# Two graph layers on one core: the prologue's order of bias rows and of the bound check's squarings

## Chip, cores and metric

The kernel runs on one NeuronCore of a Trainium2 chip. The metric is the device time of one execution in microseconds, as the median of three runs. The profile is of one further execution, taken by the hardware profiler.

## What is computed

The input `x` holds 64 samples of 256 nodes with 512 features; `adj` is one 256 x 256 adjacency matrix for all samples. Two layers follow each other, each with a layer norm and a ReLU ahead of it and a residual around it. The first is a graph attention with one head, the second an attention with eight heads of 64, masked by `adj`. All is in float32. Cut to what matters:

```python
h = maximum(layernorm(x), 0)
hw = h @ W                                   # 512 -> 256
e  = leaky_relu(hw @ a[0] + (hw @ a[1]).T, 0.2) + NEG * (1 - adj)
x  = x + concatenate([softmax(e) @ hw, hw])
h = maximum(layernorm(x), 0)
q, k, v = h @ Wq.T + bq, h @ Wk.T + bk, h @ Wv.T + bv      # 8 heads
s = where(adj == 0, -inf, q @ k.T / 8)
x = x + (softmax(s) @ v) @ Wo.T + bo
```

## The kernel before

**Tiling.** Samples go in groups of two (`GB`), so there are 32 groups (`NG`). A group's rows are four tiles of 128 rows by 512 features. While one group is in attention, the next one is projected and the one after that is in the first layer. A loop over the groups at the end of `bounded` does this, with its order written as strings of letters; ahead of it stands a prologue that brings the first groups up to that point. The change lies in the prologue (lines 1133 to 1169).

**Seven products instead of eight.** Each projection (q, k, v), and the output projection too, is done on a 2 x 2 split of its operands with seven block products and sums of blocks. So the weights need four extra blocks (`weight_sums`, line 253: T3, T1, T2, T4; T1 overwrites the block W12), and the activations three sums (`operand_sums`, line 525, on GpSimd). `projection` (line 851) issues the products in the order 1, 2, 6, 7, 5, 4, 3. They are `pq`, `pk` and `pv` in the profile, eight recorded matmuls each. ScalarE moves three of the banks on as `kept_q`, `kept_k`, `kept_v` and the last as `q`, `k` or `v`; VectorE adds three (`q<-pq,kept_q`). Product 6 accumulates onto product 1's bank, so it has to wait for the copy of that. The seventh product of k uses the bank that q's last product has been taken from.

**Norm and transposition.** `norm_T` (line 428) measures rows, makes scale and shift (`factor`, VectorE and GpSimd), normalizes on ScalarE (`xn`) and transposes. Except for the first group the transposition is done in 32 x 32 blocks by VectorE into `xt` (one buffer), then stored to DRAM (`passed<-xt`) and fetched back in four pieces (`moved<-passed`), and copied by ScalarE to `hT0` (first layer) or `hT` (second layer; both stand as `hT` in the profile). `turn` notes its last transposition in `turn_last`.

**The output bias.** The bias of v goes through the output weights: `last_bias` (line 272) has three steps. The first makes `bv_rows` on VectorE, one scaling and three multiply-adds of 128 x 512 elements, from the four unsummed blocks of `wo_sb`; its first instruction gets an edge to what `turn_last` holds. The second multiplies a matrix of ones by them on TensorE (`pb`). The third adds the result to `b_out`. GpSimd's weight sums of `wo_sb` overwrite a block that the rows read.

**The bound check.** Attention is done without subtracting a row maximum. `judge` (line 293) works out bounds of the weights' norms from which `conclude` decides whether that is allowed. Its steps are the letter "c": a Gram matrix of `wq` per head pair, one of `wk`; then the first squarings (`square_q`, `square_k`: eight recorded matmuls of 128 x 128 each), their copies back to `room` by ScalarE, and the second squarings, of which ScalarE sums the squares (`room<-square_q`). The rest follows late in the kernel.

**What sets the order.** The program is written in the wanted order, and a scheduler at build time gives each engine its fixed sequence. TensorE's is exactly that of the program: `matmul` chains every instruction to the one before (`in_order`, line 131). On the other engines `not_sooner` (line 123) ties an instruction to the engine's last one written so far. What isn't tied may be placed earlier or later by the scheduler. ScalarE's copies of q and k, its normalizations and its copies of `hT` are tied; VectorE's sums of products are not.

**The prologue's loop.** Twenty-one product steps of the first group, q, k and v mixed, are taken by `next(products)`: steps 0 to 3 (q1, q2, k1, k2) ahead of the loop, and then one for each i from 4: q6, q7, q5, q4, q3 (i = 4 to 8), k6, k7, k5, k4, k3 (9 to 13), v1, v2, v6, v7, v5, v4, v3 (14 to 20). Between them each i takes letters of `order`: "n" is a step of the third group's norms, "s" a step of the second group's first layer. At 5 there are the second group's last features (`ph`) and its score rows (`line`, `own`); at 7 its attention weights `e`; at 10 and 11 its four weighed features (`po`, two at each); at 12 and 13 the norm and transposition for its second layer; at 14 and 16 the third group's second normalization and its second transposes; at 17 and 19 the copies to `hT`. In the kernel before, the check's first squarings and copies come at 4, the second squarings at 7, the rows at 16, `pb` at 19 and its sum at 20.

Of the kernel before, what the change touches and what calls it, by code (L numbers as in the profile page):

```python
# [41 lines left out]
def two_gnn_layers(tc, *args):  # L42

    nc = tc.nc
    with tc.tile_pool(name="verdict", bufs=1) as pool:
        wrong = pool.tile([1, 1], I32, name="wrong")
        bounded(tc, *args, wrong)  # L50
        again = nc.values_load(wrong[0:1, 0:1], min_val=0, max_val=1)
        with tc.If(again > 0):
            tc.strict_bb_all_engine_barrier()
            any_inputs(tc, *args)
# [3 lines left out]
def bounded(  # L58
# [64 lines left out]
    def not_sooner(engine, operation, *args, **kwargs):  # L123

        last = engine.last
        after(getattr(engine, operation)(*args, **kwargs), last)
# [25 lines left out]
    def load(g, b):  # L152
        xs[g, b] = big.tile([P, NT, D], F32, tag="x", name=f"x{g}_{b}", bufs=8)
        if g in (2, 3):
            not_sooner(sync, "dma_start", xs[g, b], xg[g, b])
        else:
            sync.dma_start(xs[g, b], xg[g, b])
# [95 lines left out]
    def weight_sums(name, engine=vector):  # L253
        w = w_sb[name]
        not_sooner(engine, "tensor_sub", w[:, :, T3, :], w[:, :, W22, :], w[:, :, W12, :])
        engine.tensor_sub(w[:, :, T1, :], w[:, :, W12, :], w[:, :, W11, :])
        engine.tensor_sub(w[:, :, T2, :], w[:, :, W22, :], w[:, :, T1, :])
        engine.tensor_sub(w[:, :, T4, :], w[:, :, W21, :], w[:, :, T2, :])

    def first_weight_sums():  # L260
        w11, w12, w21, w22 = (
            w0_sb[:, 2 * c : 2 * c + 2, h * FH : (h + 1) * FH] for c in range(2) for h in range(2)
        )
        t2, t3, t4 = (w0_more[:, i] for i in range(3))
        not_sooner(gpsimd, "tensor_sub", t3, w22, w12)
        not_sooner(gpsimd, "tensor_sub", w12, w12, w11)
        not_sooner(gpsimd, "tensor_sub", t2, w22, w12)
        not_sooner(gpsimd, "tensor_sub", t4, w21, t2)
# [864 lines left out]
    def take(*names):  # L1133
        for name in names:
            next(work[name])
# [10 lines left out]
    take(*"n00c0n0n")  # L1146
    late_loads()
    weight_sums("q")
    take(*"uunuu0011")
    order = "nnn ssn n s - s ss ss s s n - n s - s -".split()  # L1150
    for i, parts in enumerate(order, 4):
        next(products)
        if i == 4:
            take(*"ccc")
        if i == 17:
            weight_sums("o", gpsimd)
        if i in (5, 12):
            weight_sums("kv"[i // 12])
        if i == 8 and NG > 3:
            load(3, 0)  # L1160
            load(3, 1)
        if i == 7:
            take(*"cc")
            first_weight_sums()
        for part in parts:
            if part != "-":
                next(norms if part == "n" else pieces, None)
        if i in (16, 19, 20):
            next(bias)
    additions = (piece for g in range(NG) for piece in residual(g))  # L1170

# [3 lines left out]
    for g in range(NG):  # L1175
        products = project(g + 1) if g + 1 < NG else iter(())
        pieces = first_layer(g + 2) if g + 2 < NG else iter(())
        for b, parts in enumerate(steps):
# [10 lines left out]
            i, count = -1, sum(part not in "frv" for part in parts)  # L1189
# [410 lines left out]
```

## Time and profile before

| | us |
|---|---|
| median of three runs (2403.78 to 2406.71) | 2404.09 |
| the profiled execution, its own time | 2403.24 |
| its span | 2401.6 |
| TensorE busy | 2383.5 (99%) |
| VectorE busy | 1696.1 (71%) |
| GpSimd busy | 1423.4 (59%) |
| ScalarE busy | 1021.7 (43%) |
| `bv_rows` begins / `pb` begins | 88.14 / 91.89 |
| first scores (`sc`) begin | 96.33 |

In the profile PE is TensorE, DVE is VectorE, ACT is ScalarE, POOL is GpSimd and SP is the engine that issues the DMAs. A line of the timeline gives the start, the length, the engine, the operation, what it writes and reads, the shapes and how many were merged; in brackets stands the idle time of the engine ahead of it and what ended that. The ends of matmuls are modelled and overlap, so their starts are the better measure. A line of the waits gives the waiting engine, the engine waited for, the total, the number and the longest. The granted clock of TensorE is a share of its full speed. Nearly all operations carry line 35 or 137, those of two helpers, so they are told apart by the names of their tiles.

### The profile page before, as it was taken

To read this page: it belongs to the slowest core of one execution; us is meant where nothing else is said; L and a number is where in the kernel's file an instruction comes from. 1 tells how busy PE (TensorE), PEld (TensorE's weight loads), DVE (VectorE), ACT (ScalarE), POOL (GpSimd) and SP (SyncE) were. 2 spreads that over 40 slices of the span, in tenths; PEclk is the share of its full clock that TensorE was granted. 3 is DMA by queue.
4 is the path that set the end of the run, shared out by engine and by line. 5 is a ranking of instruction groups with operands and counts; after the bars stand their busy time and mean duration, and the time that the engine had idled before them with its cause. 6 is when DMAs were issued, how large, how long until landed. Compare 5 with 4: busy or idle time off the path is not lost.

```text
span 2401.6 us, 43080 instructions
## 1 busy us (share of the span) xinstructions
PE 2383.5 (99%) x15824; PEld 2011.0 (84%) x15824; DVE 1696.1 (71%) x3346; ACT 1021.7 (43%) x2017; POOL 1423.4 (59%) x1290
## 2 busy tenths in 40 slices
PE   9899999999999999999999999999999999999998
PEld 8788888888888888888888888888888888888886
DVE  7586766776766767667767677776677676676655
ACT  4443444444443434444444434344444444343431
POOL 4465656656656565566555575555665565656552
PEclk9999999999999999999999999999999999999999
DMA  6345444544455544455444544444554445554331
GB/s 193 106 136 157 133 147 154 158 145 137 141 158 150 159 143 134 145 154 158 145 141 137 158 150 154 149 134 144 154 158 145 137 142 158 149 158 141 112 105 46
DMA packets 272041, 343.76 MB, mean 143 GB/s; under 512 B 25424, under 2 KB 217168, under 8 KB 271824
## 3 DMA queue, kind: packets, MB, share of 16 engines
q1 hardware_dynamic: 271824, 340.95, 45.9%
q8 instruction: 126, 2.06, 0.4%
q14 instruction: 91, 0.75, 0.1%
HBM read 177.22 MB, written 163.64 MB: 142 GB/s over the span
## 4 chain that ended last, share of the span: by engine, by line
PE 96%; DMA 1%; DVE 1%; ACT 0%; issue 0%; SPq 0%; POOL 0%; ACTq 0%; DVEq 0%
PE py L137 16%; PE pk L137 16%; PE pq L137 16%; PE pv L137 16%; PE sc L137 10%; PE pr L137 9%; PE ph L137 8%; PE po L137 4%; DMA adj_i<-in_adj_dram 0%; DMA moved<-passed 0%; DMA wv_sb<-in_L_gnn_Wv_dram 0%; DMA passed<-xt 0%; DVE xt L35 0%; DVE x L35 0%; ACT hT L35 0%
## 5 line engine op out<-in xcount | busy, mean ns | idle before, releaser
L35 POOL TENSOR_TENSOR p<-p 128x512 f32<-128x512 f32 x248 | 386.2, 1570 | 481.9 <-DVE p L35 464.7
L35 ACT ACTIVATE xn<-x,factor 128x512 f32<-128x512 f32 x256 | 194.8, 807 | 337.2 <-POOL factor L35 328.3
L35 DVE TENSOR_TENSOR p<-p,maskT 128x1024 f32<-128x1024 f32 x254 | 329.7, 1318 | 3.9 <-ACT p L35 3.9
L35 DVE TENSOR_TENSOR x<-py,x 128x256 f32<-128x256 f32 x448 | 185.7, 415 | 185.9 <-PE py L137 179.7
L35 ACT ACTIVATE p<-sc 128x512 f32<-128x512 f32 x512 | 257.7, 627 | 136.0 <-PE sc L137 119.1
L35 POOL TENSOR_TENSOR parts<-parts 128x512 f32<-128x512 f32 x248 | 248.1, 1000 | 84.6 <-DMA parts<-rows 62.0
L137 PE MATMUL py<-wo_sb,oT 128*128 128x256 f32 x1024 | 262.4, 379 | 0.6 <-DVE oT L35 0.6
L137 PE MATMUL sc<-q,k 64*128 64x256 f32 x2048 | 251.5, 390 | 0.3 <-ACT p L35 0.3
L137 PE MATMUL pk<-hT,wk_sb 128*128 128x256 f32 x1024 | 244.9, 382 | 1.5 <-ACT q L35 1.5
L137 PEld LDWEIGHTS sc<-q,k 64*128 64x128 f32 x2048 | 204.5, 186 | 47.9 <-issue 25.9
L137 PE MATMUL pq<-hT,wq_sb 128*128 128x256 f32 x1024 | 240.1, 382 | 1.1 <-ACT hT L35 0.7
L137 PE MATMUL pv<-wv_sb,hT 128*128 128x256 f32 x1024 | 236.8, 379 | 0.0
L137 PE MATMUL pr<-p,v 128*32 128x256 f32 x4096 | 234.2, 380 | 0.0
L137 PEld LDWEIGHTS pq<-hT,wq_sb 128*128 128x128 f32 x1024 | 191.8, 190 | 36.7 <-issue 10.3
L137 PEld LDWEIGHTS pk<-hT,wk_sb 128*128 128x128 f32 x1024 | 189.6, 190 | 35.2 <-issue 9.9
L35 POOL TENSOR_TENSOR factor<-factor,rexp 128x2 f32<-128x2 f32 (+1 forms) x132 | 117.9, 893 | 169.8 <-DVE factor L35 169.5
L137 PEld LDWEIGHTS py<-wo_sb,oT 128*128 128x128 f32 x1024 | 194.1, 190 | 28.2 <-DVE oT L35 1.1
L137 PEld LDWEIGHTS pv<-wv_sb,hT 128*128 128x128 f32 x1024 | 194.5, 190 | 26.5
L137 PEld LDWEIGHTS pr<-p,v 128*32 128x32 f32 x4096 | 126.8, 110 | 97.8 <-issue 16.6
L137 PE MATMUL py<-wo_sb,o_sums 128*128 128x256 f32 x768 | 197.6, 380 | 0.5 <-DVE x L35 0.5
L137 PE MATMUL pv<-wv_sb,sums 128*128 128x256 f32 x768 | 182.4, 380 | 0.8 <-ACT kept_v L35 0.8
L137 PE MATMUL pq<-sums,wq_sb 128*128 128x256 f32 x768 | 181.5, 379 | 0.8 <-POOL sums L35 0.8
(150 smaller groups left out, 4076.1 us busy)
## 6 DMA issues: line engine op xcount, KB each, us to landing
passed<-xt SPq DMA_DIRECT2D x124, 512.0 KB, 3.1
moved<-passed SPq DMA_DIRECT2D x496, 128.0 KB, 3.5
rows<-p SPq DMA_DIRECT2D x124, 512.0 KB, 3.4
parts<-rows SPq DMA_DIRECT2D x496, 128.0 KB, 3.0
x<-in_x_dram SPq DMA_DIRECT2D x64, 512.0 KB, 4.4
out_dram<-x SPq DMA_DIRECT2D x62, 512.0 KB, 3.9
own<-line SPq DMA_DIRECT2D x31, 256.0 KB, 3.1
wq_sb<-in_L_gnn_Wq_dram SPq DMA_DIRECT2D x2, 512.0 KB, 9.0
```

Of the source, the lines that this page charges most:

```text
L35: instruction = getattr(self.engine, operation)(*args, **kwargs)
L137: in_order(nc.tensor.matmul(*args, **kwargs))
```

## The change

Three moves within the prologue; no instruction is added or dropped.

1. The first step of `last_bias`, the rows, is taken at i = 15 instead of 16. At 15 it comes ahead of the "n" of 16, the third group's second transposes, so `turn_last` still holds the transposition of i = 13.
2. The check's first squarings (`square_q`, `square_k`) are taken ahead of the loop, directly behind two features of the second group, and so ahead of product q6. Their copies to `room` stay at 4, behind it.
3. The check's second squarings are taken at i = 11 instead of 7: behind product k5 and the first two weighed features, ahead of the last two.

```diff
-    take(*"uunuu0011")
+    take(*"uunuu0011cc")
     order = "nnn ssn n s - s ss ss s s n - n s - s -".split()
     for i, parts in enumerate(order, 4):
         next(products)
         if i == 4:
-            take(*"ccc")
+            take("c")
         if i == 17:
             weight_sums("o", gpsimd)
         if i in (5, 12):
             weight_sums("kv"[i // 12])
         if i == 8 and NG > 3:
             load(3, 0)
             load(3, 1)
+        if i == 11:
+            take(*"cc")
         if i == 7:
-            take(*"cc")
             first_weight_sums()
         for part in parts:
             if part != "-":
                 next(norms if part == "n" else pieces, None)
-        if i in (16, 19, 20):
+        if i in (15, 19, 20):
             next(bias)
```

## The prediction

> **What bounds the kernel now.** I read the page first, then the waits of TensorE for the first 260 us, then each engine's timeline there.
>
> ```profile
> PE 2383.5 (99%) x15824; PEld 2011.0 (84%) x15824; DVE 1696.1 (71%) x3346; ACT 1021.7 (43%) x2017; POOL 1423.4 (59%) x1290
> ```
>
> TensorE is busy for 99% of the span, and the chain that ended last is 96% PE. What an edit of the prologue can win is therefore time in which PE stands still there, and a microsecond won at 100 us is kept to the end as long as no new wait opens. The waits are few:
>
> ```profile
> PE pb L137 <- DVE bv_rows L35: 5.6, 1, 5.6
> PE pk L137 <- ACT q L35: 1.5, 1, 1.5
> ...
> PE pq L137 <- POOL sums L35: 0.8, 1, 0.8
> PE pv L137 <- ACT kept_v L35: 0.8, 1, 0.8
> ```
>
> The timeline of PE places them (start, length, the wait in brackets):
>
> ```profile
> 44.72 1.99 PE L137 MATMUL pq<-sums,wq_sb 128*128 128x256 f32 x8 [0.83 <-POOL sums L35]
> 46.55 1.05 PE L137 MATMUL square_q<-room 128*128 128x128 f32 x8
> ...
> 57.01 1.05 PE L137 MATMUL square_q<-room 128*128 128x128 f32 x8
> 57.90 1.06 PE L137 MATMUL square_k<-room 128*128 128x128 f32 x8
> 58.79 1.89 PE L137 MATMUL pq<-sums,wq_sb 128*128 128x256 f32 x8
> 60.52 1.89 PE L137 MATMUL pk<-sums,wk_sb 128*128 128x256 f32 x8
> 63.95 1.99 PE L137 MATMUL pk<-hT,wk_sb 128*128 128x256 f32 x8 [1.53 <-ACT q L35]
> ...
> 84.39 1.89 PE L137 MATMUL pv<-wv_sb,hT 128*128 128x256 f32 x8
> 91.89 2.08 PE L137 MATMUL pb<-bv_rows,square_ones 128*128 128x512 f32 x2 [5.61 <-DVE bv_rows L35]
> 93.75 2.65 PE L137 MATMUL pv<-wv_sb,sums 128*128 128x256 f32 x8
> 96.33 3.92 PE L137 MATMUL sc<-q,k 64*128 64x256 f32 x32
> ```
>
> Starts 1.73 us apart are an eight-piece product at full pace. After the long wait it is slower (93.75 to 96.33 is 2.58). The reason for the long wait is VectorE's order:
>
> ```profile
> 79.74 1.29 DVE L35 STREAM_TRANSPOSE xt<-xn 128x512 f32<-128x512 f32 x2
> 84.66 0.69 DVE L35 TENSOR_TENSOR v<-pv,kept_v 128x512 f32<-128x512 f32 x1 [3.63 <-PE pv L137]
> 86.32 0.69 DVE L35 TENSOR_TENSOR v<-pv,kept_v 128x512 f32<-128x512 f32 x1 [0.96 <-PE pv L137]
> 86.92 1.29 DVE L35 STREAM_TRANSPOSE xt<-xn 128x512 f32<-128x512 f32 x2
> 88.14 0.45 DVE L35 TENSOR_SCALAR bv_rows<-wo_sb,bv_col 128x512 f32<-128x512 f32 x1
> ```
>
> The rows stand behind the third group's second transposes (86.92), while VectorE has 3.63 us free from 81.03.
>
> [...] the granted clock falls at 88.45, 2.2 us into the wait, and returns at 95.28, 6.83 us[...] later. [...] ACT's copy of q stands behind the whole attention chain and starts at 63.07, when that ends at 63.16. [...] The last of the four row instructions takes 1.63 us beside GpSimd's weight sums, the two before it 0.75.
>
> **Part 1, the rows one step sooner.** It removes the edge to the transposes of 86.92 and leaves one to those of 79.74. Nothing is added: the four instructions (0.45 + 2 x 0.75 + 1.63, from 88.14 to 91.85 = 3.7 us) move into VectorE's gap, and with them, earlier, GpSimd's three sums of wo_sb that wait for them. Their inputs landed long ago. At the old pace they would end at 81.03 + 3.7 = 84.7; pb is wanted at 84.39 + 1.73 = 86.12. The stall goes: 91.89 - 86.12 = 5.77. The slow clock behind it goes too: pb and one product take 96.33 - 91.89 = 4.44; at full pace 0.86 (pb streams as many columns as half a product) + 1.73 = 2.59; so 1.85. Sum **7.6 us**. No DMA is in this step. Queued behind the rows on VectorE are v's sums (84.66 and 86.32); the last v product needs the bank that the first of them reads, but comes after pb, so 1.6 late is still in time. The store and the loads of the third group's transposes keep their places on SP's queue; if the rows do push those transposes, by 3.7 at most, their operand copies on ACT (106.45) have some 10 us in hand after the loads issued at 88.72. What is late next I come to under part 3.
>
> **Part 2, the first squarings ahead of q's sums.** The 0.83 us wait at 44.72 is for GpSimd; the squarings (16 pieces, 46.55 to 48.34 = 1.79) are ready and fill it. The product then starts at 43.72 + 1.79 = 45.51 and the next ends at 48.97 instead of 50.07: 1.1 us. But ACT has kept_q, two room copies and then hT in fixed order; kept_q follows that product, so starts at 47.4 instead of 46.76, and the first hT copy ends near 47.4 + 0.84 + 2 x 0.55 + 0.6 = 49.9. The features that read it (50.07) can start at 49.95. Bounds 0 to 1.1; I take **0.1**, that is nothing: the wait goes from GpSimd's sums to hT.
>
> **Part 3, the second squarings behind the weighed features.** They were 1.79 us of work ahead of the 63.95 wait, and that wait is not set by PE. It ends with ACT's copy of q, behind the exponentials (61.74 to 63.16), behind own's landing at 60.05, behind the features. ACT loses its two squarings (58.16 to 59.75) but was idle 0.34 for the DMA before e, so the chain does not move. PE now reaches the wait at 62.25 - 1.78 = 60.47 and stands still 3.48 us instead of 1.7. Two costs follow.
> - *The work itself*, now after the wait, ahead of the last two weighed features. These start 1.78 later, and VectorE, which was full from 66.84 to 81.03, idles for them: its reciprocal would come at 72.08 (1.06 after the features, as at 65.78 and 66.84) instead of 70.51, 1.5 later. Then factor, xn, k, kept_v shift by up to 1.53 and the product of 78.81 starts at 80.34; PE alone would be there at 77.88 + 1.78 = 79.66, a shift of 0.85. Between these I take **1.2**. ACT's two squarings (0.6 each and 0.2 to read a sum) now stand ahead of its xn (71.89, which waits for GpSimd's factor until then); they would run between 70 and 72, so xn may lose some 0.2, which the bounds cover. No DMA belongs to these steps.
> - *The clock*. [...] The record has a window with 1.53 idle that kept full clock, and one with 2.17 idle (86.28 to 88.45) that lost it. So the clock most likely halves around 64, for one window: half of 3.41 us, **1.7**. Bounds 0 and 3.4[...].
>
> *What is late next*: the scores. VectorE's transposes of 79.74 feed a store, a load and ACT's hT copy: 81.03 to 90.18, 9.15 us, then v's copy (0.6) and the exponentials. With the transposes shifted by 1.2 to 1.5 the exponentials can start at 92.0 at the soonest, where the scores come at 86.12 + 1.2 + 2.6 = 89.9; they hold five banks and need the first back after two pairs, at 92.0; the first exponential ends at 92.6. Bounds 0 to 1; I take **0.5**. GpSimd's sums, which waited for PE until 96.55, start near 91.3 and are in time.
>
> **Sum.** 7.6 + 0.1 - 1.2 - 1.7 - 0.5 = 4.3. From the profiled execution (2403.24; its span is 2401.6 and 1.6 lies around it) 2399.0. The median of before, 2404.09, is 0.85 above that execution[...]. The kernel after has such a spread too, so I add nothing.
>
> **Rivals.**
> - *No halved clock at the new wait*[...]: 2399.0 - 1.7 = 2397.3. For it: the 1.53 wait kept full clock. Against: the wait is twice as long. Chance 0.25.
> - *More given back*: two slow windows, or the full 1.53 and a full microsecond at the scores: 2399.0 + 1.7 + 0.8 = 2401.5. For it: VectorE has no slack from 66.84 to 81.03. Against: PE has work without a break from 64 on[...]. Chance 0.13.
> - *Slower: the rows don't move.* Only an edge is taken away; the place is the scheduler's. If VectorE still has the rows behind the transposes of 86.92, the 7.6 are not won and the squarings' price remains: 2403.24 + 1.5 + 1.7 to 3.4 = 2406.4 to 2408.1. It decides once the rows end later than about 90. Against: VectorE has nothing else ready from 81 to 84.7. Chance 0.05.
>
> **Numbers.** The forecast has 0.54, with 2397.9 to 2400.8 around it; an order of the scheduler that I don't foresee has 0.03, on the slow side. 0.2% is 4.8 us, about what a measurement of this kernel can tell from no change, so the border is 2399.3, close to the forecast: faster is two thirds of the forecast's chance (0.36) and all of the first rival's, 0.61; slower by over 0.2%, from 2408.9 on, is the unforeseen order and the upper end of the last rival[...], 0.05; the rest of the forecast (0.18), the second rival and most of the last one lie within, 0.34. The range, 2396.6 to 2402.0, leaves out the last rival and the ends of two.
>
> **What would show it.** Right: bv_rows directly behind the transposes near 80 to 82; no pb wait in PE's list; the pq wait replaced by one of ph for hT of up to a microsecond; pk's wait for q near 3.5 us with a clock record below 1 around 64 to 68; square_q near 69; the product after kept_v near 80 to 82; full clock from there on; scores near 90 to 92. Wrong: rows behind 86; pk starting well before 63.5; a wait after 100 us that isn't there now, for hT0's sums or parts, which would mean that another chain takes the gain.

## Result and profile after

The changed kernel takes 2408.48 us (median of 20 runs, 2405.52 to 2410.62), the kernel before 2403.62 in the 20 runs beside it: ratio 1.0018, 95% interval 1.0011 to 1.0025. The medians lie 4.9 us apart, to the slow side (the ratio makes 4.3 of it), where 4.3 faster was forecast; the time lies 6.5 us above the range. Its profiled execution took 2408.41, with a span of 2406.8 against 2401.6.

The waits of TensorE, in the same 260 us as before:

```profile
PE sc L137 <- ACT p L35: 4.9, 1, 4.9
PE ph L137 <- POOL sums_xn L35: 2.8, 1, 2.8
PE pk L137 <- ACT q L35: 2.8, 1, 2.8
...
PE ph L137 <- ACT hT L35: 0.7, 1, 0.7
```

The wait of `pb` is gone, as it should be, and that of `pq` for GpSimd's sums has become one of `ph` for `hT`. The two at the head are new. PE's timeline places them:

```profile
63.38 2.71 PE L137 MATMUL pk<-hT,wk_sb 128*128 128x256 f32 x8 [2.83 <-ACT q L35]
...
81.47 1.99 PE L137 MATMUL pv<-wv_sb,sums 128*128 128x256 f32 x8 [0.52 <-ACT kept_v L35]
...
88.78 1.02 PE L137 MATMUL pb<-bv_rows,square_ones 128*128 128x512 f32 x2
...
91.46 3.92 PE L137 MATMUL sc<-q,k 64*128 64x256 f32 x32
...
107.50 1.95 PE L137 MATMUL ph<-w_sb,hT 128*128 128x129 f32 x16
112.29 2.09 PE L137 MATMUL ph<-w_more,sums_xn 128*128 128x129 f32 x8 [2.85 <-POOL sums_xn L35]
...
118.52 3.62 PE L137 MATMUL pk<-hT,wk_sb 128*128 128x256 f32 x16
...
135.57 4.62 PE L137 MATMUL sc<-q,k 64*128 64x256 f32 x21 [4.90 <-ACT p L35]
...
140.33 1.99 PE L137 MATMUL pk<-sums,wk_sb 128*128 128x256 f32 x8
```

The same products in the kernel before:

```profile
112.98 1.95 PE L137 MATMUL ph<-w_sb,hT 128*128 128x129 f32 x16
...
119.25 3.62 PE L137 MATMUL pk<-hT,wk_sb 128*128 128x256 f32 x16
...
129.85 1.56 PE L137 MATMUL sc<-q,k 64*128 64x256 f32 x10
...
134.44 1.99 PE L137 MATMUL pk<-sums,wk_sb 128*128 128x256 f32 x8
```

Follow the gain along it, each start against the same product of before. At the first scores it is 96.33 - 91.46 = 4.87. At the third group's features (`ph`), which begin at 107.50 instead of 112.98, it is 5.48. From there to the next `pk` the kernel before took 6.27 and this one 11.02 (107.50 to 118.52): 4.75 lost. From the second scores to the `pk` behind them it is 4.59 and 11.22 (129.11 to 140.33): 6.63 lost. 5.48 - 4.75 - 6.63 = -5.90, and the products of `pr` that stood at 161.42 stand at 167.31. So all of the loss arises in two places between 107 and 140 us, and nothing is lost after that (at the end the spans differ by 5.2). Each place has a wait and, behind it, PE at half clock: the mean granted clock is 0.57 from 112 to 116 and 0.55 from 136 to 140. The stretches of the span, with the granted clock ahead of the two DMA columns:

```profile
64.00:68.00 4.00, 4.00 (x13) 3.18 (x12) 0.16 (x1) 0.90 (x3) 0.00 (x0) 0.57 0.03 9
...
112.00:116.00 4.00, 3.71 (x18) 3.71 (x19) 0.00 (x0) 0.37 (x1) 3.92 (x5) 0.57 0.43 140
...
136.00:140.00 4.00, 4.00 (x21) 3.19 (x20) 3.93 (x8) 2.39 (x4) 0.00 (x0) 0.55 0.01 4
```

The rows are where the change wants them, directly behind the transposes that they are still tied to, and ahead of the third group's second ones (VectorE's timeline):

```profile
82.39 1.29 DVE L35 STREAM_TRANSPOSE xt<-xn 128x512 f32<-128x512 f32 x2
83.61 0.45 DVE L35 TENSOR_SCALAR bv_rows<-wo_sb,bv_col 128x512 f32<-128x512 f32 x1
...
90.44 1.29 DVE L35 STREAM_TRANSPOSE xt<-xn 128x512 f32<-128x512 f32 x2
```

What leads to the two waits is read from the chain that ended last (start, length, what):

```profile
107.70 0.03 ACT q L35
...
108.93 0.64 ACT hT L35
109.64 1.27 POOL sums_r L35
...
122.24 0.09 DVE k L35
...
122.85 0.45 DVE parts L35
...
125.59 2.76 DMA line<-rows
...
128.82 3.08 DMA passed<-xt
...
131.94 1.71 ACT e L35 x4
```

ScalarE copies the second half of the third group's `hT` only after it has taken `q`. It begins that at 107.70, when q's last product is done, and has stood idle for 3.32 us ahead of it. GpSimd's sums start behind the copy, and `ph` waits for them. Further down, VectorE transposes the first row parts at 122.85, only after k's sum at 122.24, though GpSimd had finished them at 116.7; the fetch of the next parts stands behind that on SyncE's queue, `line` and `own` behind the fetch, `e` behind `own`, and the exponentials of the scores behind `e` on ScalarE. The chain names the store `passed<-xt` ahead of `e`. But `e` reads `own`, which was issued just ahead of that store, at 128.43, and landed 3.4 us later, by the start of `e`; the store took 4.3.

Neither order was in the kernel before. The instruction lists of the two built programs show it (unchanged lines left out), and the order of starts in the two traces agrees:

```diff
 ScalarE
 kept_q<-pq_1 (product 1), kept_q<-pq_1 (product 6)
-hT_2_0<-moved_2_0
-hT_2_1<-moved_2_1
 kept_q<-pq_1 (product 7)
+hT_2_0<-moved_2_0
 q_0<-pq_1
+hT_2_1<-moved_2_1
 VectorE
-parts_0_0, compact_0
 H<-ph_2 (product 4), rows, ..., k_0<-pk_1
+parts_0_0, compact_0
```

A third difference, ScalarE's copy of the second group's second half amid the first scores' exponentials instead of ahead of them, did no harm: the scores at 91.46 run without a wait. Apart from what the edits themselves move, and two small `factor` steps of VectorE ahead of a reciprocal, the traces show no other. GpSimd's and SyncE's lists are the same as before.

The copies of `hT` (line 520) and the transposes of the parts (line 1010) are tied. What is not tied is what now stands ahead of them: VectorE's sums of H and k, and ScalarE's takings of the second group's q. Of the latter the text on the kernel before says that they are tied; by `behind` in `take` this holds for the first group alone (`g == 0`).

### The profile page after: what moved, and what is told of

Read it like the earlier page. It is cut to its first block, busy times and chain, and to the rows that moved or that the text cites. A ratio compares the mean times of both kernels' runs of the same rounds, so it can differ in the third digit from the quotient of the medians.

```text
span 2406.8 us, 43080 instructions
## 1 busy us (share of the span) xinstructions
PE 2386.7 (99%) x15824; PEld 2014.5 (84%) x15824; DVE 1687.7 (70%) x3346; ACT 1020.9 (42%) x2017; POOL 1420.4 (59%) x1290
## 4 chain that ended last, share of the span: by engine, by line
PE 97%; DMA 1%; DVE 1%; ACT 0%; SPq 0%; issue 0%; POOL 0%; DVEq 0%; ACTq 0%
PE pq L137 16%; PE pk L137 16%; PE py L137 16%; PE pv L137 16%; PE sc L137 10%; PE pr L137 9%; PE ph L137 8%; PE po L137 5%; DMA adj_i<-in_adj_dram 0%; DMA wv_sb<-in_L_gnn_Wv_dram 0%; DMA line<-rows 0%; ACT e L35 0%; PE total L137 0%; PE gram_q L137 0%; PE gram_k L137 0%
## 5 line engine op out<-in xcount | busy, mean ns | idle before, releaser
L35 DVE TENSOR_TENSOR p<-p,maskT 128x1024 f32<-128x1024 f32 x254 | 323.4, 1294 | 2.0 <-ACT p L35 2.0
L137 PE MATMUL pk<-sums,wk_sb 128*128 128x256 f32 x768 | 181.5, 379 | 0.0
```

The lines of the kernel that those rows point to most:

```text
L35: instruction = getattr(self.engine, operation)(*args, **kwargs)
L137: in_order(nc.tensor.matmul(*args, **kwargs))
```

## Experiments

**Theory.** The three edits cost and bring what was worked out, up to the scores. The loss is that of the order in which the scheduler then lays out other, untied instructions: `kept_q` and `q` ahead of ScalarE's copies of the third group, and the sums of H and k ahead of VectorE's row parts. **Rival.** The late waits come from the squarings' shift and the slow clock at 64, or from another chain that can't keep up with an earlier PE whatever the order.

**The edits one by one.** The kernels of the experiments are numbered e1 to e10. The first here (e1) has only `(16, 19, 20)` changed to `(15, 19, 20)`; the second (e2) only the move of the second squarings from 7 to 11; the last (e10) only the first squarings.

> The rows one step sooner and nothing else; the squarings stand as in the kernel before. Theory (order): with the rows ahead, the scheduler puts ScalarE's copies of the third group's hT behind kept_q and q, and VectorE's sum of the first row parts behind k's sum; the instruction lists of this kernel already have both. So the pb wait is gone and the first scores begin near 88.7 (7.6 sooner), but features then wait near 107 for GpSimd's sums (about 2.9) and scores near 130 for ScalarE (about 4.9), with slow clock behind both; some 2.8 us better than the changed kernel, as the k wait stays short: 2405.7, slower than before by about 2. Rival (the late waits come from the squarings' shift and the slow clock at 64): no wait of over a microsecond after 100 us, and 2396 to 2397.

Measured: 2406.62 us (13 runs) beside 2403.77, ratio 1.0009 (1.0000 to 1.0017). The scores begin at 88.81, all of the 7.5 us won; `ph` then waits 2.85 and `sc` 4.85. The rows alone bring both late waits, without any squaring moved. The first rival falls.

> The second squarings behind the weighed features and nothing else. By the prediction's price: k's wait for q grows from 1.5 to about 3, the clock halves for one window (1.7), the later work shifts by about 1.2, and the pb wait stays: 2403.6 + 2.9 = 2406.5 with no wait after 100 us that the kernel before lacks. Order theory: the same, since the lists after the scores are those of before. Rival (the squarings' shift causes the late waits): waits of 2.8 and 4.9 near 110 and 131 appear, and 2410 or more.

Measured: 2405.63 (13 runs) beside 2403.77, ratio 1.0008 (0.9999 to 1.0016). `pk` waits 3.01, behind it `pk` and `po` run slow (5.25 us, 63.25 to 68.50, for 3.56 in the kernel before), the scores begin at 99.08, 2.75 later than before, and no later wait exceeds 0.34. So up to the scores this edit costs about what was worked out, and it doesn't make the late waits. Its whole time is 1.9 above that of before, 0.9 less than expected, and the interval just includes no change.

> The first squarings ahead of q's sums and nothing else; the lists of all engines but TensorE's are those of the kernel before. Part 2 says 0.1: 2403.8 within the scatter, and no wait after 100 us that the kernel before lacks. If the first squarings upset anything behind: over 2405.

Measured: 2403.58 (13 runs) beside 2403.08, ratio 1.0002 (0.9994 to 1.0010): nothing that can be told from zero. Its profiled execution was one of the slowest (2406.04): behind the wait for `q` of 1.99 the granted clock was 0.68 from 64 to 68, where it was 1.00 in the profiled execution of before, and `pk` and `po` took 5.25 (64.47 to 69.72) instead of 3.56.

**The changed kernel again** (e3):

> The changed kernel once more, for one look beside the others: 2408.5, a wait of sc for p near 4.9 and of ph for sums_xn near 2.8.

Measured: 2407.97 in its one run, waits of 5.6 and 2.9. So the two waits came again in a second execution.

**The copies tied.** This is the changed kernel (e4), with one line of `projection` (`take`) altered, so that the takings of the second group's q come behind what was written before them:

```diff
-            behind = [scalar.last] if g == 0 and name != "v" else []
+            behind = [scalar.last] if (g == 0 and name != "v") or (g == 1 and name == "q") else []
```

This puts ScalarE's copies back ahead of product 7's `kept_q`, and the scheduler then puts VectorE's parts back too, though no edge asks for it.

> The changed kernel, with ScalarE's takings of the second group's q products tied to the instruction written before them, so that the copies of the third group's hT come ahead of kept_q and q as in the kernel before. The lists of VectorE, SyncE and GpSimd then are those of before again, but for the rows. Theory (order): the waits of ph for sums_xn and of sc for p vanish, the gain at the scores is kept: 2399.0 to 2399.5, the number that was predicted. Rival (delay and clock): both waits stay, 2407 to 2409.

Measured: 2399.31 (14 runs) beside 2403.77, ratio 0.9980 (0.9972 to 0.9988). ScalarE's copies, all four at once, and the waits in this kernel:

```profile
101.42 2.17 ACT L35 COPY hT<-moved 128x512 f32<-128x512 f32 x4
```

```profile
PE sc L137 <- ACT p L35: 0.8, 1, 0.8
...
PE ph L137 <- POOL sums_xn L35: 0.6, 1, 0.6
```

The copies follow the `kept_q` before them without idle time, so their loads had landed: nothing on the chip asked for the later place. With one line of ties changed, 9.2 us come back (2408.48 to 2399.31). The second rival, that another chain can't follow, falls with it: what is left of it is 0.8 and 0.6. The same ties on the rows alone (e5):

> The rows one step sooner, with the takings of the second group's q products tied as in e4; the squarings stand as before. ScalarE's list differs from that of the kernel before only in one pair of copies that stands amid the exponentials. Order theory: the whole gain of the rows is kept, as the scores begin 2.5 sooner than in e4 (88.8 against 91.3): 2399.3 - 2.5 = 2396.8. Rival (another chain takes what comes sooner): the waits for sums_xn and for p, 0.55 and 0.82 in e4, grow by what is won, and the time stays at 2399.

Measured: 2396.28 (6 runs) beside 2403.82, ratio 0.9969 (0.9956 to 0.9981), the lowest median of all these kernels; scores at 88.87, waits behind them of 0.5 at most. With the first squarings moved too (e9):

> e5 with the first squarings ahead of q's sums too; the second squarings stay where they were. The prediction's part 2 says 0.1, so 2396.3, with the wait of pq for GpSimd's sums turned into one of ph for hT. Then the 3.0 between e4 and e5 belong to the second squarings alone. If the first squarings have a price of their own: 2397 to 2399.

Measured: 2397.15 (10 runs) beside 2403.08, ratio 0.9976 (0.9967 to 0.9986). The interval overlaps that of the kernel without them, so no price of the first squarings is shown in the time. But both profiles with them show `e` later than the one without (60.6 beside 60.1 in e10 and before, 60.7 beside 60.1 in e9 and e5), and in e10 k's seventh product is 0.52 later (64.47 beside 63.95). `own` took 4.4 and 4.5 us to land there, beside 3.9 and 4.1, and both medians lie higher, by 0.5 and 0.9. A price of about half a microsecond would fit all of this, but two pairs of executions don't show that the squarings cause the later landing. The second squarings, the difference of e4 and e9, cost 1.5 us if each is taken from the runs of before beside it (2.2 from the medians alone), and not 3.0.

**The order without the edits.** This is the kernel before (e6), with two letters "n" of one string written later, so that only ScalarE's four copies move, to the changed kernel's places:

```diff
-                parts = "Smmnfuuumnmnuufuussssfsfssuvnfrunnfsuu"
+                parts = "Smmnfuuummunufuunssssfsfssuvnfrunnfsuu"
```

> The kernel before, with the two steps that copy the third group's hT written later, so that ScalarE does them behind kept_q and behind q, as in the changed kernel. Nothing else differs in any list of an engine. Order theory: from e1 and e4 the order costs 2406.6 - (2399.3 - 2.5) = 9.8 us together with VectorE's order; with ScalarE's alone the wait of ph for sums_xn (2.9) and whatever the slow clock adds come, and the parts reach VectorE as late as GpSimd lets them: 2403.8 + 3 to 10, thus 2407 to 2413. Rival (the order only hurts when everything is earlier): 2404, no new wait.

Measured: 2408.37 (21 runs) beside 2403.82, ratio 1.0018 (1.0011 to 1.0025), by chance the very ratio of the change under study, with none of its edits. Its waits, ahead of and behind the `pb` wait that it still has:

```profile
PE ph L137 <- POOL sums_xn L35: 2.9, 1, 2.9
...
PE sc L137 <- ACT p L35: 0.5, 1, 0.5
```

The late copies alone make the wait of `ph`, in a kernel that runs as late as before. They don't make the wait of `sc`. No half clock followed the wait of `ph` in this execution (the granted clock is 1.00 from 108 to 124), which took 2406.58, 1.8 less than the median.

**The two orders apart.** This is the changed kernel (e7) with H's and k's sums tied, so that the row parts come ahead of them again, and ScalarE's copies left late:

```diff
+        if g == 2:
+            not_sooner(vector, "tensor_add", part(1, 0), second, p16)
...
+        if (g, name) == (1, "k"):
+            not_sooner(vector, "tensor_add", part(0, 0), second, p1)
```

> The changed kernel, with two sums of VectorE tied so that the sum of the first row parts again comes ahead of H's and k's sums, while ScalarE's copies keep their late place. It tells the two orders apart. If VectorE's order makes the wait of sc for p: that wait falls from 4.9 to under 1, the wait of ph for sums_xn (2.9) stays, and the time is 2408.3 - 4.9 - 1.7 to 3.4 of slow clock = 2400 to 2401.7. If the late copies make both: the wait for p stays above 3 and the time is 2407 to 2408.

Measured: 2402.63 (13 runs) beside 2403.82, ratio 0.9991 (0.9983 to 0.9999), a little over the first case's 2401.7. `ph` still waits, `sc` hardly:

```profile
PE ph L137 <- POOL sums_xn L35: 2.9, 1, 2.9
...
PE sc L137 <- ACT p L35: 0.8, 1, 0.8
```

One pair of ScalarE's `kept_k` also moved in this list, behind that wait of `ph`. So VectorE's order made the wait of `sc`: 2408.48 - 2402.63 = 5.85 us with its slow clock. ScalarE's made that of `ph`: 2402.63 - 2399.31 = 3.3. These shares are what comes back one after the other; the late copies alone cost 4.55 in e6 (2408.37 - 2403.82).

**The clock at the k wait.** This is the tied kernel again (e8), with idle matmuls ahead of k's seventh product:

```diff
+        if i == 9:
+            idle = mm("idle")
+            for _ in range(13):
+                matmul(idle[:, :P], square_ones, square_ones, start=True, stop=True)
```

> e4 with 13 idle matmuls of 128 x 128 on a bank that nobody reads, ahead of k's seventh product (2.9 us of work for a wait of 3.0). They add no result. If the half window of slow clock behind that wait costs 1.7: the clock record shows no half speed between 60 and 80, k's products run at full pace from 63.4, and the time is 2399.3 - 1.7 = 2397.6. If the clock there is hidden by VectorE, which is full behind it: 2399.3 within 0.5.

Measured: 2398.94 (19 runs) beside 2403.82, ratio 0.9979 (0.9972 to 0.9986), 0.4 below the tied kernel's median, which the scatter doesn't tell from nothing; by the number this is the second case. The profiles do show the effect: without the idle matmuls it takes 17.93 from k's seventh product to the v product behind `kept_v` (63.38 to 81.31), with them 16.41 (63.80 to 80.21), so 1.5 less at full clock (`pk` and `po` take 3.57, 63.80 to 67.37, instead of 5.09), and the scores begin 1.1 sooner (90.19 for 91.29). The other 0.4 went to the wait itself, which ended later: `own` took 4.2 us to land instead of 3.3. For the median the price of this one slow stretch stays open.

## Why the prediction was wrong

*Part 1, right to the scores.* The rows stand at 83.61, `pb` at 88.78 has no wait, and with the rows alone the scores begin 7.5 sooner (96.33 to 88.81), for 7.6 worked out. The estimate of 0.86 for `pb` at full clock came out too (88.78 to 89.64).

*Part 2, right within the scatter.* The waiting product of q starts behind the squarings, at 45.60, and `ph` waits 0.68 for `hT` in its place. The time of this edit alone is that of before. That `e` came about half a microsecond later in both pairs of profiles was not foreseen.

*Part 3, right in mechanism, off in sizes that cancel.* In the changed kernel the wait for `q` is 2.83 (2.98 as the prediction measured it, from 60.40, where a product at full pace ends), not 3.48: the chain to it ended 0.57 sooner. The record of the clock shows half speed from 64.52 to 67.93, 3.41 us; `pk` and `po` take 5.25 (63.38 to 68.63) instead of 3.56, so 1.7, as taken. The 3.41 of the prediction, its "window", is half of the 6.83 for which the clock was low in the profile of before (88.45 to 95.28); that it would be low here too, and for one such half, was an estimate. From k's seventh product to the v product behind `kept_v` it is 18.09 against 14.86 (63.95 to 78.81): 3.23, of which the clock explains 1.7 and the shifted work 1.5, the upper bound, where 1.2 was taken. The kernel with the idle matmuls confirms it: at full clock it takes 16.41, 1.55 more than before. No wait came at the first scores, where 0.5 was taken. There ScalarE's copy had moved in among the exponentials, so that they didn't have to follow it; that this spared the wait was not tried. GpSimd's sums, put near 91.3, began at 95.78 behind this copy and were still in time. Together the scores should have begun at 89.9 + 1.7 = 91.6, or 92.1 with the 0.5; they did at 91.46. That this comes so close is in part luck.

*The step that failed* is the one from the scores to the end: "a microsecond won at 100 us is kept to the end as long as no new wait opens", with the list of what might be late. I went through the engines with the orders that the profile of before showed, and let the new order be the scheduler's only for the rows ("Only an edge is taken away; the place is the scheduler's"). For the copies of `hT` I counted "some 10 us in hand after the loads". The loads did have that time. It didn't matter, because the copies ran where ScalarE's list has them (it stood idle for 3.32 us ahead of `q`, with the copy behind that), and the rows' move had changed that list, and VectorE's, 20 to 40 us further on. The takings of the second group's q and the sums of H and k were free to move ahead of tied work. This term stood at nothing in the sum, and it measured 9.2 us: 5.85 by VectorE's order and 3.3 by ScalarE's. The text ends with the right sign to look for, "a wait after 100 us that isn't there now, for hT0's sums or parts", but gives it no price, and an unforeseen order of the scheduler a chance of 0.03. The forecast number itself, 2399.0, is what the same three edits give with these two orders as before (2399.31), helped by the sizes that cancel.

*The slower rival* supposed that the rows wouldn't move. They did; the time it gave, up to 2408.1, agrees only by accident.

*What stays open.* Why the scheduler chose the other places isn't shown by any run; its own estimates of time aren't in these profiles. With ScalarE's order restored by ties (e4), VectorE's came back of itself. But ScalarE's copies went late without VectorE's change (e6), and VectorE's order could be held while the copies stayed late (e7). So one doesn't simply follow from the other, and why the two came together stays open. What put the copy amid the exponentials wasn't tried.

## What to carry to other kernels

Where a scheduler lays out what isn't tied, an edit of one step is an edit of every untied sequence behind it. Compare the instruction lists of both programs, engine by engine, before a gain is carried to the end; two changes of order cost 9.2 us here, more than the edit had won. And tie what the tuned order depends on; read in the code what really is tied: with one line of ties changed the same edit turned from 4.9 us slower to 4.5 faster, and its best part alone from 2.9 slower to 7.5 faster.

## What the runs showed of the hardware

- *Behind waits of two to six microseconds TensorE often ran at half clock, but not always.* In the profile of before the record of the clock shows 0.50 from 88.45 to 95.28 (6.83 us), within the `pb` wait of 5.61 and behind it. In the changed kernel it shows 0.50 from 64.52 to 67.93 (3.41), from 112.30 to 115.72 (3.41) and from 132.78 to 139.61 (6.83), behind the waits of 2.83 and 2.85 and within that of 4.90. In the 3.41 us ahead of these four falls TensorE was idle for 2.17, 2.27, 2.85 and 2.11 us. Of ten waits between 2.78 and 3.01 us (for `q` and for `sums_xn`, in seven profiles), eight were followed by slow products: `pk` took 2.71 to 3.66 behind the five for `q`, where it takes 1.99 at full clock, and the slowest eight matmuls of `ph` took 1.93 to 2.09 behind three of those for `sums_xn`, instead of 1.06. The two others, of 2.85 in e3 and e6, kept full clock (1.00 from 108 to 124). Of the four of 1.53 to 1.88, none was followed by a slow product (`pk` took 1.99 each time). One of 1.99 was (e10, where `pk` took 2.87); behind one of 2.1 the mean granted clock of the execution is 1.000 (e9). So the length of the wait alone doesn't tell; what decides it is not shown.
- *The executions with more half clock were the slower ones.* Of the 20 executions of the changed kernel, nine had a mean granted clock of 0.998 and a median time of 2407.22 us, eight 0.997 and 2408.66, three 0.996 and 2410.47. So a part of the scatter goes with the share of half clock.
- *The same transfer takes 3.3 to 4.5 us to land.* `own<-line` took 3.3 to 3.5 in the five profiles (of four kernels) with the second squarings moved and nothing put in their place, and 3.9 to 4.5 in the seven others, the one with idle matmuls among them. This gave the changed kernel back about half a microsecond at the k wait (3.4 beside 3.9 in the kernel before), which nobody had counted. What causes it wasn't tried.
